# A four-layer graph network on one core: another order for the first full round of the attention ring, and for VectorE's opening

## The chip, the cores and the metric

One core of a Trainium2 chip runs the whole network in one launch. The metric is the device time of a run in microseconds (us). Engines are named as the profile names them: PE (TensorE, with PEld for its weight loads), DVE (VectorE), ACT (ScalarE), POOL (GpSimd) and SP (SyncE, which here only issues DMAs). Each engine executes its own queue strictly in order; an instruction that waits holds up everything behind it on that engine and nothing on the others.

## The reference, cut to what matters

Input x has shape (128, 64, 256): 128 graphs of 64 nodes with 256 features, and one 64x64 adjacency for all. Four layers follow each other, each of the form x = x + layer(relu(layernorm(x))):

```python
# layer 0: aggregation with the normalized adjacency, then two products with batch norms
A_norm = A + I;  dinv = rsqrt(row sums + column sums - diagonal)
agg = (A_norm * dinv[:, None] * dinv[None, :]) @ h
out = batchnorm(relu(batchnorm(agg @ W1.T + b1)) @ W2.T + b2)
# layer 1: two graph convolutions, then LSTMs over windows of 1, 2, 3 and 4 nodes
# layer 2: causal attention with one head of 256, adjacency added to the scores
# layer 3: attention with 4 heads of 64, masked where the adjacency is 0; the output keeps its layout
```

All is float32.

## The kernel before, in words

The 8192 rows of x are cut into 16 chunks of 512 rows (four tiles of 128 rows and 256 features). Layer 0 goes over the chunks twice (the batch norms need sums over all chunks), layer 1 over pairs of chunks. Layers 2 and 3 are one software pipeline, which the code calls a ring: while chunk c is in layer 2, chunk c-2 gets its projections in layer 3 and chunk c-3 its softmax. This study touches two places: the opening, and the first full round of that ring.

**The opening** (lines 376 to 409). A manual schedule: all five engines execute in the order in which the code is written. The adjacency and the first two chunks of x are loaded; the first chunk comes in two halves, one issued by SP (L382) and one by ACT (L383). `degrees` (L119 to L122) makes the row sums on DVE; `rsqrt` (L99, L100) makes dinv on POOL. `normalized` scales the rows by dinv on DVE (L129), transposes them on PE (L131) and scales again on DVE into `ahat_t` (L132). `ln_stats` takes each tile's mean and variance on DVE (L159, L160) and the inverse deviation on POOL (L99, L100); `ln_apply` makes the shift `nmr` on DVE (L172) and normalizes on ACT, tile by tile, into `hs` (L174). `aggregate0` multiplies `hs` by `ahat_t` on PE (L201) and copies one half of the result on DVE (L332) and one on ACT (L334). `product1` makes the first product on PE (L347), copies it out on ACT (L349) and takes the batch norm's sums on DVE (L350). `keep_busy` issues transposes of the identity on PE whose results nobody reads (L151). `product1(0)` aggregates the second chunk halfway (L341). From the second chunk on only PE's order is written by hand; that of the other engines is made by the planner that compiles the kernel, from the dependences and its own due times.

**The ring** (lines 1519 to 1561). Each order is a string of steps, `step+k` or `step-k`, run for chunk c+k or c-k; again all five engines follow the order of the string. `FIRST` starts the pipeline with chunks 0 to 2, `ROUND` is one full round, `NORM` and `LAST` end it. The first full round is c = 3. The steps of this study:

- `q2` projects the chunk's queries in two products (L1108); the first half is copied by ACT (L1169), the second by DVE in `copyq2` (L1174). `v2a`, `v2b` and `v3a`, `v3b` project the values (L1101) and copy them by ACT (L1103). `score2` multiplies them (L1191); DVE adds the mask (L1194) and takes the maxima (L1115), POOL subtracts (L1116), ACT exponentiates in `exp2` (L1201). `divide2` is three DVE instructions (L1120, L1125, L1126), `turn2` transposes on PE (L1135) with a copy by ACT (L1139), `out2` multiplies by the values (L1222), and DVE adds to x (L1225).
- `norm3`, `apply3`, `square3`, `load3`: the layer norm's moments on DVE with `rsqrt` on POOL; the shift on DVE (L172) and the normalization on ACT (L174); a transposition in four DVE instructions (L259) that SP writes to DRAM (L234); and SP's reading back (L241), which turns the chunk to channels.
- `qa`, `q5`, `qb`, `qc`, `qd` are seven products for queries and keys (L1297, Strassen's form), accumulated in three PSUM banks X, Y, Z. Bank X is used four times: `qa` copies it by ACT (L1312), `qb` adds to it and copies (L1326), `qc` adds to it and DVE adds it to `qk` (L1336), `qd` adds to it and ACT copies (L1341). Each addition to X waits until the reader before it is done. `c11`, `c12` are DVE's additions of Z and Y. `sums_h` makes four sums of operands on POOL (L674 to L677), after POOL made the sums of the weights in `ring_places` (L1276).
- `exp3`, `sum3`, `divide3`, `turn3`, `out3` are the softmax of layer 3 and its product (L1404, L1120, L1125 and L1126, L1135, L1424); `score3` its scores (L1376, masks L1382).

Of the kernel before, what the change touches and what calls it, by code (L numbers as in the profile page):

```python
# [19 lines left out]
def kernel(  # L20
# [22 lines left out]
    nc = tc.nc  # L43
# [13 lines left out]
    SUP = 2  # L57
# [28 lines left out]
    def bank(name, tag="ps"):  # L86
        return psum[0][0].tile([P, CH], F32, tag=tag, name=name, bufs=psum[0][1][tag])
# [9 lines left out]
    def rsqrt(dst, src, eps):  # L97

        nc.gpsimd.tensor_scalar(dst, src, eps, None, op0=OP.add)  # L99
        nc.gpsimd.tensor_tensor(dst, dst, mhalf[:, : dst.shape[1]], OP.pow)  # L100
# [7 lines left out]
    ahat_t = const.tile([P, P], F32, name="ahat_t")  # L108
# [18 lines left out]
    def normalized(setup, an, dinv):  # L127
        rows = setup.tile([P, P], F32, name="rows")
        nc.vector.tensor_scalar(rows, an, dinv, None, op0=OP.mult)  # L129
        pt = bank("pt_ahat")  # L130
        nc.tensor.transpose(pt[:, :P], rows, ident)  # L131
        nc.vector.tensor_scalar(ahat_t, pt[:, :P], dinv, None, op0=OP.mult)  # L132

    def masks(setup):
        causal = setup.tile([P, P], F32, name="causal")
# [11 lines left out]
    def keep_busy(n, name):  # L147

        ps = bank(f"idle_{name}")
        for i in range(n):  # L150
            nc.tensor.transpose(ps[:, :P], ident, ident)  # L151


    def ln_stats(src, name, tiles=range(NJ)):
        n = len(tiles)
        st = small.tile([P, n, 6], F32, tag=f"ln_st{n}", name=f"st_{name}")
        mv = small.tile([P, n, 2], F32, tag=f"ln_mv{n}", name=f"mv_{name}")
        for i, j in enumerate(tiles):
            nc.vector.bn_stats(st[:, i, :], src[:, j, :])  # L159
            nc.vector.bn_aggr(mv[:, i, :], st[:, i, :])  # L160
        rstd = small.tile([P, n], F32, tag=f"ln_rstd{n}", name=f"rstd_{name}")
        rsqrt(rstd, mv[:, :, 1], EPS)
        return mv, rstd

    def ln_apply(dst, src, mv, rstd, name, tiles=range(NJ), by_pool=False):
        n = len(tiles)
        nmr = small.tile([P, n], F32, tag=f"ln_nmr{n}", name=f"nmr_{name}")
        if by_pool:
            nc.gpsimd.tensor_tensor(nmr, mv[:, :, 0], rstd, OP.mult)
            nc.gpsimd.tensor_scalar(nmr, nmr, -1.0, None, op0=OP.mult)  # L170
        else:
            nc.vector.scalar_tensor_tensor(nmr, mv[:, :, 0], -1.0, rstd, op0=OP.mult, op1=OP.mult)  # L172
        for i, j in enumerate(tiles):
            nc.scalar.activation(dst[:, j, :], src[:, j, :], AF.Relu, bias=nmr[:, i : i + 1],  # L174
                                 scale=rstd[:, i : i + 1])
# [15 lines left out]
    def aggregate(src, mat, name):  # L191

        banks = [bank(f"agg{e}_{name}").rearrange("p (k j t) -> p k j t", j=NJ, t=T) for e in range(2)]
        for j in range(NJ):
            for k in range(KD):
                for i in range(2):
                    for e in range(2):
                        f = slice(k * P + i * T, k * P + (i + 1) * T)  # L200
                        nc.tensor.matmul(banks[e][half(i), k, j, :], src[half(e), j, f],  # L201
                                         mat[half(e), half(e)], start=True, stop=True)
        return [ps.rearrange("p k j t -> p (k j) t") for ps in banks]
# [105 lines left out]
    setup, close_setup = pool("setup", 1, "right")  # L309
# [17 lines left out]
    def aggregate0(c):  # L327
        aggs[c] = l0.tile([P, KD, CH], F32, tag="agg", name=f"agg_{c}")
        dst = aggs[c].rearrange("p k (j e t) -> p e (k j) t", e=2, t=T)
        for e, ps in enumerate(aggregate(hs.pop(c), ahat_t, f"a{c}")):  # L330
            if e == 0:
                nc.vector.tensor_copy(dst[:, e], ps)  # L332
            else:
                nc.scalar.copy(dst[:, e], ps)  # L334
# [39 lines left out]
    with tc.manual_schedule(engines={mybir.EngineType.PE, mybir.EngineType.DVE,  # L374
                                     mybir.EngineType.Activation, mybir.EngineType.Pool,
                                     mybir.EngineType.SP}):
        for e in range(2):
            r = slice(e * T, (e + 1) * T)
            nc.sync.dma_start(adj_bd[r, r], adj)
            nc.scalar.dma_start(adjt_bd[r, r], adj_t)  # L380
        xts = [l0.tile([P, NJ, D], F32, tag="xt", name=f"xt_{c}", bufs=3) for c in range(2)]
        nc.sync.dma_start(xts[0][:, : NJ // 2], xr[0][:, : NJ // 2])  # L382
        nc.scalar.dma_start(xts[0][:, NJ // 2 :], xr[0][:, NJ // 2 :])  # L383
        nc.gpsimd.dma_start(w1_sb, w1t.rearrange("(k p) f -> p k f", p=P))
        nc.sync.dma_start(xts[1], xr[1])
        for c in range(2):
            hs[c] = l0.tile([P, NJ, D], F32, tag="h", name=f"h_{c}")
        nc.sync.dma_start(bn1_sb, bn1)
        others = setup.tile([P, P], F32, name="others")
        nc.vector.tensor_scalar(others, ident, -1.0, 1.0, op0=OP.mult, op1=OP.add)  # L390
        dinv = degrees(setup, others)
        keep_busy(34, "a")

        parts = [range(2 * i, 2 * i + 2) for i in range(2)]
        stats = [ln_stats(xts[0], "a00", parts[0])]
        an = setup.tile([P, P], F32, name="an")
        nc.vector.tensor_add(an, adj_bd, ident)
        normalized(setup, an, dinv)
        keep_busy(10, "b")
        stats.append(ln_stats(xts[0], "a01", parts[1]))  # L400
        for i in range(2):
            ln_apply(hs[0], xts[0], *stats[i], f"a0{i}", parts[i])
        mv, rstd = ln_stats(xts[1], "a1")
        aggregate0(0)
        ln_apply(hs[1], xts[1], mv, rstd, "a1")
        keep_busy(8, "c")
        xt = load0(2)
        stats2 = xt, *ln_stats(xt, "a2")
        product1(0)
# [563 lines left out]
    st, steps = {}, {}  # L973
# [530 lines left out]
    def store(c, t):  # L1504
# [3 lines left out]
        for r in range(2):  # L1508
# [5 lines left out]
    ROUND = """exp3-3 q2+0 copyq2+0 sum3-3 load3-1 sums_h-2 load2+1 v2a+0 divide3-3 score2+0 exp2+0 v2b+0  # L1514
               divide2+0 turn3-3 qa-2 turn2+0 q5-2 c11-2 out2+0 keep+0 norm3a+0 qb-2 back-2 qc-2 norm3b+0 c12-2
               v3a-2 qd-2 apply3+0 out3-3 score3-2 store-3 square3+0 v3b-2"""

    NORM = """exp3-3 q2+0 copyq2+0 sum3-3 load3-1 sums_h-2 v2a+0 divide3-3 score2+0 exp2+0 v2b+0 norm2+1
              divide2+0 turn3-3 qa-2 turn2+0 q5-2 c11-2 out2+0 keep+0 norm3a+0 qb-2 apply2+1 back-2 qc-2
              norm3b+0 c12-2 v3a-2 chan2+1 qd-2 apply3+0 out3-3 score3-2 store-3 square3+0 v3b-2"""  # L1520
# [5 lines left out]
               score2+1 norm3+0 exp2+1 q2+2 divide2+1 copyq2+2 apply3+0 back+0 v2a+2 v2b+2 turn2+1  # L1526
               score2+2 chan3+0 pair1+14 pair1+14 out2+1 keep+1 exp2+2 divide2+2 q30+0 k30+0 turn2+2
               norm3+1 pair1+15 pair1+15 q31+0 k31+0 apply3+1 out2+2 keep+2 square3+1 score3+0 norm3+2
               v3a+0 load3+1 v3b+0 apply3+2 square3+2"""
    LAST = """exp3-2 sum3-2 load3+0 divide3-2 qa-1 q5-1 c11-1 v3a-1 qb-1 c12-1 qc-1 turn3-2 out3-2 qd-1  # L1530
              q30+0 score3-1 store-2 back-1 k30+0 back+0 exp3-1 q31+0 k31+0 sum3-1 divide3-1 score3h+0
              v3b-1 exp3a+0 sum3a+0 turn3-1 exp3b+0 v3a+0 divide3a+0 out3-1 sum3b+0 divide3b+0 store-1
# [3 lines left out]
    def run(order, c):  # L1536
        for name in order.split():
            i = max(name.find("+"), name.find("-"))
            steps[name[:i]](c + int(name[i:]))

    with tc.manual_schedule(engines={mybir.EngineType.PE, mybir.EngineType.DVE,
                                     mybir.EngineType.Activation, mybir.EngineType.Pool,
                                     mybir.EngineType.SP}):
        run(FIRST, 0)
        close_l1r()
        pool3, close_l3 = pool("l3", 2, "right")
        l3.append(pool3)
# [58 lines left out]
```

## Time and profile before

| | us |
|---|---|
| median of 8 runs | 1925.62 (1923.12 to 1927.42) |
| the profiled execution's own time | 1926.83 |
| its span, first to last instruction | 1925.1 |
| PE busy in the span | 1901.7 (99%) |
| DVE busy | 1159.2 (60%) |
| ACT busy | 958.3 (50%) |
| POOL busy | 413.1 (21%) |

The mean granted clock of TensorE over the span is 0.998 of full speed. A row of the timeline has the start in us from the span's start, the duration (of merged instructions from the first start to the last end), engine, line, operation, tiles, shapes and count, and in brackets how long the engine had been idle and what ended that. Matmuls are pipelined: a row's end lies some 0.1 to 0.2 us behind the start of the row that follows it without a gap, so distances on PE are taken from start to start.

### The profile page before, as it was taken

To read this page: it belongs to the slowest core of one execution; us is meant where nothing else is said; L and a number is where in the kernel's file an instruction comes from. 1 tells how busy PE (TensorE), PEld (TensorE's weight loads), DVE (VectorE), ACT (ScalarE), POOL (GpSimd) and SP (SyncE) were. 2 spreads that over 40 slices of the span, in tenths; PEclk is the share of its full clock that TensorE was granted. 3 is DMA by queue.
4 is the path that set the end of the run, shared out by engine and by line. 5 is a ranking of instruction groups with operands and counts; after the bars stand their busy time and mean duration, and the time that the engine had idled before them with its cause. 6 is when DMAs were issued, how large, how long until landed. Compare 5 with 4: busy or idle time off the path is not lost.

```text
span 1925.1 us, 38314 instructions
## 1 busy us (share of the span) xinstructions
PE 1901.7 (99%) x14979; PEld 1464.5 (76%) x14979; DVE 1159.2 (60%) x3019; ACT 958.3 (50%) x2132; POOL 413.1 (21%) x613
## 2 busy tenths in 40 slices
PE   9999999999999999999999999999999999999998
PEld 5444465897897889699689789878969967777776
DVE  6644354546557656755755764665555566677776
ACT  5655434445455455455545645545554544444453
POOL 3204210221211221121121121112113113233332
PEclk9999999999999999999999999999999999999999
DMA  4116712224424521532632452353144244444433
GB/s 135 60 40 221 276 53 66 83 83 163 155 83 148 180 95 64 178 103 91 194 135 83 159 181 83 104 184 107 56 143 131 87 150 137 133 141 147 143 111 111
DMA packets 110500, 240.36 MB, mean 125 GB/s; under 512 B 11376, under 2 KB 74352, under 8 KB 110320
## 3 DMA queue, kind: packets, MB, share of 16 engines
q1 hardware_dynamic: 109568, 236.57, 36.9%
q8 instruction: 119, 1.95, 0.4%
q0 software_dynamic: 320, 1.05, 0.2%
q14 instruction: 61, 0.50, 0.1%
q10 hardware_dynamic: 432, 0.30, 0.0%
HBM read 169.98 MB, written 67.90 MB: 124 GB/s over the span
## 4 chain that ended last, share of the span: by engine, by line
PE 95%; DVE 3%; ACT 1%; issue 1%; POOL 0%; DMA 0%; SPq 0%; DVEq 0%; POOLq 0%; ACTq 0%
PE x L829 22%; PE g L793 18%; PE z L829 11%; PE z L347 6%; PE y L829 6%; PE z L364 6%; PE v L1101 5%; PE p_q L1108 3%; PE u L574 3%; PE v L560 3%; PE X L1297 3%; PE Y L1297 1%; PE agg_a L201 1%; PE agg_c L201 1%; PE s L1191 1%; PE agg_b L201 1%
## 5 line engine op out<-in xcount | busy, mean ns | idle before, releaser
L838 DVE TENSOR_TENSOR gates<-gates,x 128x128 f32<-128x128 f32 (+2 forms) x384 | 119.5, 322 | 335.4 <-PE x L829 328.4
L829 PE MATMUL x<-xd,wset 128*128 128x128 f32 (+2 forms) x1280 | 285.6, 311 | 0.4 <-DVE gates L838 0.2
L829 PE MATMUL x<-hd,wset 128*128 128x128 f32 (+2 forms) x1152 | 247.2, 303 | 0.0
L829 PEld LDWEIGHTS x<-xd,wset 128*128 128x128 f32 x1280 | 202.4, 190 | 17.5 <-DVE gates L838 3.9
L887 POOL TENSOR_TENSOR gates<-gates 128x512 f32<-128x512 f32 (+2 forms) x48 | 74.9, 1560 | 648.1 <-ACT gates L721 648.1
L721 ACT ACTIVATE gates<-gates,bias 128x256 f32<-128x256 f32 (+4 forms) x384 | 170.4, 491 | 67.0 <-DVE gates L838 64.3
L829 PEld LDWEIGHTS x<-hd,wset 128*128 128x128 f32 x1152 | 185.3, 191 | 4.9
L772 ACT ACTIVATE gates<-g,bias 128x512 f32<-128x512 f32 (+2 forms) x240 | 138.0, 609 | 98.0 <-PE g L793 94.7
L793 PE MATMUL g<-hT,wset 128*128 128x256 f32 (+2 forms) x744 | 184.5, 405 | 1.2 <-DVE hT L732 1.1
L793 PEld LDWEIGHTS g<-hT,wset 128*128 128x128 f32 x744 | 140.9, 190 | 43.8 <-issue 8.8
L793 PE MATMUL g<-hT,wih 128*128 128x512 f32 x384 | 166.4, 593 | 0.0
L835 ACT COPY gates<-y 128x128 f32<-128x128 f32 (+2 forms) x192 | 54.1, 293 | 205.4 <-PE y L829 204.9
L829 PE MATMUL z<-hs,wset 128*128 128x128 f32 (+2 forms) x768 | 154.3, 303 | 0.0
L793 PEld LDWEIGHTS g<-hT,wih 128*128 128x128 f32 x384 | 72.5, 191 | 87.5 <-issue 83.1
L829 PEld LDWEIGHTS z<-hs,wset 128*128 128x128 f32 x768 | 119.9, 191 | 3.3
L347 PE MATMUL z<-agg,w_sb 128*128 128x512 f32 x256 | 114.1, 599 | 0.1
L778 DVE TENSOR_TENSOR cell<-gates 128x512 f32<-128x512 f32 (+2 forms) x80 | 50.4, 647 | 101.4 <-ACT gates L772 101.3
L364 PE MATMUL z<-h,w_sb 128*128 128x512 f32 x256 | 110.2, 593 | 0.0
L838 DVE TENSOR_TENSOR gates<-gates,z 128x128 f32<-128x128 f32 (+2 forms) x384 | 104.8, 317 | 0.1
L835 ACT COPY gates<-x 128x128 f32<-128x128 f32 (+2 forms) x192 | 56.5, 295 | 93.9 <-PE x L829 93.1
L721 ACT ACTIVATE gates<-x,bias 128x128 f32<-128x128 f32 (+2 forms) x192 | 74.7, 389 | 50.9 <-PE x L829 48.0
L829 PE MATMUL z<-hT,wset 128*128 128x128 f32 (+1 forms) x512 | 97.0, 302 | 0.0
(243 smaller groups left out, 3646.5 us busy)
## 6 DMA issues: line engine op xcount, KB each, us to landing
wset<-wfar SPq DMA_DIRECT2D x96, 960.0 KB, 6.4
hT<-far_h SPq DMA_DIRECT2D x124, 128.0 KB, 2.9
far_h<-hm SPq DMA_DIRECT2D x16, 512.0 KB, 3.7
far_n<-xs SPq DMA_DIRECT2D x16, 512.0 KB, 6.8
xs<-far_n SPq DMA_DIRECT2D x64, 128.0 KB, 3.3
far_x<-xs SPq DMA_DIRECT2D x16, 512.0 KB, 3.0
x<-far_x SPq DMA_DIRECT2D x64, 128.0 KB, 3.2
xt<-in_x_dram SPq DMA_DIRECT2D x15, 512.0 KB, 4.0
```

The costliest lines, as they stand in the source:

```text
L201: nc.tensor.matmul(banks[e][half(i), k, j, :], src[half(e), j, f], mat[half(e), half(e)], start=True, stop=True)
L347: nc.tensor.matmul(ps, w1_sb[:, k, m * P : (m + 1) * P], agg[:, k, :], start=(k == 0), stop=(k == KD - 1))
L364: nc.tensor.matmul(banks[c, m], w2_sb[:, k, m * P : (m + 1) * P], h1[c][:, k, :], start=(k == 0), stop=(k == KH - 1))
L721: nc.scalar.activation(gate(q, c, part), src, AF.Tanh if q == 2 else AF.Sigmoid, bias=bs[:, q * KD + c : q * KD + c + 1])
L772: nc.scalar.activation(columns_of(gate(q, c)), natural(banks[q, c][:, :n].rearrange("p (w b) -> p w b", b=nb)), AF.Tanh if q == 2 else AF. ...
L793: nc.tensor.matmul(banks[q, c][:, :n].rearrange("p (w b) -> p w b", b=nb)[:, w, :], block(q, c, k), hv[:, k, w.start * p : (w.stop - 1) * ...
L829: nc.tensor.matmul(folded(self.psum(kind)), wsets[p, self.q][:, BLOCKS[kind][i], :], (ox[self.s] if part == "x" else oh)[kind], start=firs ...
L835: nc.scalar.copy(gate(self.q, kind // 5, halves[kind // 5]), self.psum(kind))
L838: nc.vector.tensor_add(gate(self.q, *dst), gate(self.q, *a), self.psum(kind))
L887: nc.gpsimd.tensor_mul(gates[:, 0, :, :n], gates[:, 0, :, :n], gates[:, 2, :, :n])
L1101: nc.tensor.matmul(ps[:, i, :], hT[:, k, j, :], w[:, k, first : first + D], start=(k == 0), stop=(k == KD - 1))
L1297: nc.tensor.matmul(st[c, tag][:, i * CH // 2 : (i + 1) * CH // 2].rearrange("p (a n) -> p a n", n=P), w, st[c, "o7"][kind], start=first an ...
```

## The change

Two edits.

In the opening, the second half of the first chunk gets its moments from a generator, `ln_moments`, which does what `ln_stats` does but can be stopped after each tile. One tile's moments now come before `an` (L396) and the scaled rows, the other behind them. `normalized` returns the PSUM bank of its transposition, and the last scaling into `ahat_t` is issued behind the first `ln_apply`. `keep_busy` "b" issues 12 transposes instead of 10. The moments of the second chunk are taken in two halves, one before the aggregation of the first chunk and one behind it, and applied in two halves.

In the ring, `apply3` and `square3` of chunk 2 leave the end of `FIRST`. Round c = 3 gets an order of its own, `THIRD`, in place of `ROUND` with its first three steps permuted: there `apply3` of chunk 2 stands behind `copyq2`, `square3` behind `exp2`, `load2` of chunk 4 ahead of the writing back of `square3`, `sum3`, `load3` and `sums_h` behind `score2` and `exp2`, `turn3` behind `qa`, and `v3a` of chunk 1 behind `qa` instead of behind `c12`.

```diff
+    def ln_moments(src, name, tiles):
+        n = len(tiles)
...
+        for i, j in enumerate(tiles):
+            nc.vector.bn_stats(st[:, i, :], src[:, j, :])
+            nc.vector.bn_aggr(mv[:, i, :], st[:, i, :])
+            yield
+        rstd = small.tile([P, n], F32, tag=f"ln_rstd{n}", name=f"rstd_{name}")
+        rsqrt(rstd, mv[:, :, 1], EPS)
+        yield mv, rstd
...
         stats = [ln_stats(xts[0], "a00", parts[0])]
+        late = ln_moments(xts[0], "a01", parts[1])
+        next(late)
         an = setup.tile([P, P], F32, name="an")
         nc.vector.tensor_add(an, adj_bd, ident)
-        normalized(setup, an, dinv)
-        keep_busy(10, "b")
-        stats.append(ln_stats(xts[0], "a01", parts[1]))
+        pt = normalized(setup, an, dinv)
+        keep_busy(12, "b")
+        next(late)
+        stats.append(next(late))
+        ln_apply(hs[0], xts[0], *stats[0], "a00", parts[0])
+        nc.vector.tensor_scalar(ahat_t, pt[:, :P], dinv, None, op0=OP.mult)
+        ln_apply(hs[0], xts[0], *stats[1], "a01", parts[1])
+        stats = [ln_stats(xts[1], "a10", parts[0])]
+        aggregate0(0)
+        stats.append(ln_stats(xts[1], "a11", parts[1]))
         for i in range(2):
-            ln_apply(hs[0], xts[0], *stats[i], f"a0{i}", parts[i])
-        mv, rstd = ln_stats(xts[1], "a1")
-        aggregate0(0)
-        ln_apply(hs[1], xts[1], mv, rstd, "a1")
+            ln_apply(hs[1], xts[1], *stats[i], f"a1{i}", parts[i])
...
+    THIRD = """q2+0 copyq2+0 apply3-1 exp3-3 load2+1 v2a+0 score2+0 exp2+0 square3-1 sum3-3 load3-1 sums_h-2
+               v2b+0 divide3-3 divide2+0 qa-2 v3a-2 turn3-3 turn2+0 q5-2 c11-2 out2+0 keep+0 norm3a+0 qb-2
+               back-2 qc-2 norm3b+0 c12-2 qd-2 apply3+0 out3-3 score3-2 store-3 square3+0 v3b-2"""
...
-               v3a+0 load3+1 v3b+0 apply3+2 square3+2"""
+               v3a+0 load3+1 v3b+0"""
...
-        run(ROUND.replace("exp3-3 q2+0 copyq2+0", "q2+0 copyq2+0 exp3-3"), SUP + 1)
+        run(THIRD, SUP + 1)
```

More of the change, by code (lines that the diff above doesn't have):

```diff
@@ L131, in normalized @@
         nc.tensor.transpose(pt[:, :P], rows, ident)
-        nc.vector.tensor_scalar(ahat_t, pt[:, :P], dinv, None, op0=OP.mult)
+        return pt
     def masks(setup):
@@ L163, in ln_stats @@
         return mv, rstd
+    def ln_moments(src, name, tiles):
+        n = len(tiles)
+        st = small.tile([P, n, 6], F32, tag=f"ln_st{n}", name=f"st_{name}")
+        mv = small.tile([P, n, 2], F32, tag=f"ln_mv{n}", name=f"mv_{name}")
+        for i, j in enumerate(tiles):
[5 more added lines that the diff above has]
+        yield mv, rstd
     def ln_apply(dst, src, mv, rstd, name, tiles=range(NJ), by_pool=False):
```

## The prediction

> **What bounds the kernel.** I read first the page's table of engines, then the windows around the ring's start, then the timeline there, then the opening. The table says that PE is busy in 99% of the span:
>
> ```profile
> PE 1901.7 (99%) x14979; PEld 1464.5 (76%) x14979; DVE 1159.2 (60%) x3019; ACT 958.3 (50%) x2132; POOL 413.1 (21%) x613
> ```
>
> So only PE's 23.4 us of idleness (1925.1 - 1901.7), and time in which it is slow, can be won. The windows (length, busy time of PE, PEld, DVE, ACT, POOL, granted clock, DMA share, GB/s) find both at the first full round:
>
> ```profile
> 1590.00:1597.00 7.00, 4.05 (x17) 2.35 (x15) 3.75 (x12) 3.68 (x7) 6.66 (x10) 0.92 0.25 75
> 1597.00:1603.00 6.00, 6.00 (x43) 5.07 (x44) 4.33 (x8) 0.99 (x3) 1.78 (x3) 0.53 0.63 201
> ...
> 1615.00:1638.00 23.00, 23.00 (x274) 17.71 (x275) 16.20 (x34) 10.50 (x20) 6.57 (x8) 1.00 0.46 139
> ```
>
> PE loses 2.95 us to idleness, and then runs at a granted clock of 0.53. The shortfalls of both windows, (0.08 x 7 + 0.47 x 6) x 2, make some 6.8 us at half clock. The next round (third line) has neither. The timeline shows the cause:
>
> ```profile
> 1591.68 1.89 PE L1101 MATMUL v<-wvo_sb,hT 128*128 128x256 f32 x8
> ...
> 1592.48 0.72 POOL L1276 TENSOR_TENSOR ws<-w_sb 128x256 f32<-128x256 f32 x1
> 1592.54 0.68 DVE L172 SCALAR_TENSOR_TENSOR nmr_n<-mv_n,rstd_n 128x4 f32<-128x4 f32 x1 [1.47 <-POOL rstd_n L100]
> ...
> 1593.32 2.07 ACT L174 ACTIVATE h<-xs,nmr_n,rstd_n 128x256 f32<-128x256 f32 x4 [4.29 <-DVE nmr_n L172]
> ...
> 1594.93 1.43 DVE L259 STREAM_TRANSPOSE mid<-h 128x256 f32<-128x256 f32 x4 [1.71 <-ACT h L174]
> 1595.30 0.56 ACT L1169 COPY q<-p_q 128x512 f32<-128x512 f32 x1
> ...
> 1596.28 0.65 DVE L1174 COPY q<-p_q 128x512 f32<-128x512 f32 x1
> ...
> 1596.99 1.98 PE L1191 MATMUL s<-hT,q 128*64 128x64 f32 x30 [0.60 <-DVE q L1174]
> ```
>
> The scores wait for the two copies of q2, and these stand, on ACT behind apply3 and on DVE behind square3, both of chunk 2, whose shift waits for POOL. Their product was ready long before (its eight matmuls start at 1588.24).
>
> **The ceiling in the ring.** From the start of q2's products to that of v3b, PE takes 26.60 us here (1588.24 to 1614.84) and 20.50 in the next round (1616.67 to 1637.17). Of the difference of 6.10, 4.26 have arisen by the start of v2b (10.65 against 6.39), 1.75 between v2b and turn3 (half clock, 3.58 against 1.83), 0.09 later.
>
> **The round with the new order.** The starts up to 1588.24 stay. ACT's copy of q2 falls to about 1590.0, copyq2 to 1591.7 (0.04 after the product's end), so the scores start behind v2a at 1593.5 without a wait, and v2b at 1594.6. apply3 keeps its time: its shift waits for POOL until 1592.5 in both versions. qa and v3a fill PE from 1596.5 to 1599.9 (0.87 + 0.86 + 1.73). DVE meanwhile: mask and maxima to 1595.7 (0.42 each), square3 to 1597.1 (1.43), sum3 to 1598.3 (1.21), reciprocal to 1598.6 (0.25), then the multiplication of 1.23 (these are the durations of the same instructions before). Undisturbed it would end at 1599.86, just in time for turn3 at 1599.92.
>
> It is disturbed. POOL now subtracts the second layer's maxima (to 1596.4) ahead of sums_h, whose four additions (0.72 to 0.73 each, 2.90 from 1595.34 to 1598.24 before) move to 1596.4 to 1599.3. The shift at 1592.54 took 0.68 instead of the usual 0.15 to 0.16 and ended 0.02 after POOL's addition beside it; both read two operands from SBUF. The multiplication of divide3 also reads two. I let it wait for the last addition: end at 1600.53, **turn3 0.68 late**. The bounds are 0 and 0.85 (one addition, plus the margin that I may have misplaced). [...]
>
> divide2 follows (0.42 + 0.18 + 0.43) and holds turn2 for another **0.16**. ACT's copies for out2 then end in time; the 0.10 that the next round loses at that place is in the 20.50 and comes back.
>
> v3a is gone from between qc and qd. What it hid:
>
> ```profile
> 1609.19 1.11 PE L1297 MATMUL X<-td,ws 128*128 128x256 f32 x4
> ...
> 1610.13 1.89 PE L1101 MATMUL v<-w_sb,hT 128*128 128x256 f32 x8
> ...
> 1610.40 0.69 DVE L1336 TENSOR_TENSOR qk<-qk,X 128x512 f32<-128x512 f32 x1 [0.52 <-PE X L1297]
> ```
>
> qd writes to bank X, which DVE reads until 1611.09. Without v3a it could start at 1610.13, and it will start at about 1611.16: **1.03 lost**. The bounds are 0 and 1.73, v3a's length. Behind qd on PE wait out3, score3 and v3b, that is, the rest of the round.
>
> The DMAs: load2 of chunk 4 goes out at about 1592 instead of 1601, four issues ahead of the write of square3, which waits for DVE until 1597.1 (before 1596.39). Its reading back lands some 8 us later (1596.39 to 1602.6 and a landing of 2.9 before), against a need at about 1615, when sums_h of the next round starts. SP's keep, back and store stand behind it as before. I cost this at nothing; without that margin of some 9 us it would be paid one to one.
>
> Gain in the ring: 6.10 + 0.10 - 0.68 - 0.16 - 1.03 = **4.33**. The rounds behind it are bound by PE, so it lasts to the end.
>
> **The opening.** PE's end of the aggregation and DVE's copy set the first product:
>
> ```profile
> 14.16 1.09 PE L151 MATMUL idle_c<-ident 128*128 128x128 f32 x8
> ...
> 14.65 0.66 DVE L332 COPY agg<-agg_a 128x512 f32<-128x512 f32 x1
> ...
> 15.41 3.67 PE L347 MATMUL z<-agg,w_sb 128*128 128x512 f32 x8
> ```
>
> In the new order one tile's moments (0.52) push the scaled rows from 9.16 to 9.68; the transposition starts at 10.02, and the 12 idle transposes (0.108 each) end at 11.5, beside the normalization. The last tile's moments end at 10.63 instead of 11.30, the rsqrt for it at 11.71 instead of 12.40, so ACT normalizes the last two tiles at 11.94 instead of 12.63, and PE ends 0.69 earlier. Two of the second chunk's tiles no longer stand ahead of DVE's copy, which gives 0.16 more: the first product starts at 14.56, **0.85** earlier.
>
> Little of that lasts. Three chunks on, PE waits for the normalization of chunk 3:
>
> ```profile
> 31.08 2.07 ACT L174 ACTIVATE h<-xt,nmr_a,rstd_a 128x256 f32<-128x256 f32 x4 [1.83 <-POOL nmr_a L170]
> ...
> 31.89 1.78 PE L201 MATMUL agg_a<-ahat_t,h 64*64 64x64 f32 x64
> ```
>
> The aggregation takes 1.71 there, from start to start, instead of 1.09, paced by ACT. That normalization hangs on DVE without a break since 23.95, and that on the batch norm's sums of the first product (19.09), ACT-bound before. In the new order DVE waits for POOL's rsqrt of the second half (until 16.6; before 16.21), then does the 2.21 us of chunk 2's moments, and starts those sums at 18.93: 0.16 earlier. So I count **0.16** of the 0.85; the bounds are -0.5 (DVE's wait for POOL 0.5 longer than I place it) and 0.85 (the planner, which orders DVE from the second chunk on, finds another order).
>
> **Sum.** 4.33 + 0.16 = 4.49. Against the profiled execution, 1926.83 (1.73 around its span of 1925.1), that is 1922.3; that execution is 1.21 above the median, and from the median it is **1921.1**.
>
> **Rivals.** (1) DVE's chain and bank X cost nothing and the opening's gain lasts: 6.10 + 0.85 = 6.95, 1918.7. For it: DVE meets turn3 within 0.1 without POOL. Against it: X's accumulation waits in this very round (0.21 for the copy of L1326). Chance 0.20. (2) The clock. Half clock cost 1.75 + 0.77 (scores, 1.90 instead of 1.13) = 2.52 of the 6.10. If the median run lacks it, the gain is 4.49 - 2.52 = 1.97, 1923.7; if the new waits bring it, 6.83 x 0.5 = 3.41 are lost, 1924.5. For it: the runs before spread over 4.3 us. Against it: the new gaps are 0.68 and 1.03, apart by 5 us. [...] Chance 0.15. (3) The wait moves to turn3: DVE's chain there is 1.5 later than I place it, which PE pays one to one: 4.49 - 1.5, 1922.6. Chance 0.12. (4) Slower: the planner's order for layer 0 shifts with the opening, and each later chunk's normalization comes late. From chunk 4 on it is 4.4 us early (ACT ends at 36.3, PE needs it at 40.7), so lateness must pass 4.4; each us beyond costs 12 chunks 12 us. It decides from 5.1: 0.7 x 12 = 8.4 lost, 1929.5; at 5.5 it is 13.2, 1934.3. Nothing but the planner's freedom speaks for it. Chance 0.03. The forecast has 0.50, with 1920.0 to 1922.4 as its own range.
>
> **Range and chances.** What a measurement of this kernel can tell from no change is about 0.2%, 3.85 us: faster means below 1921.77. About three quarters of the forecast lie there (0.37) and all of (1): 0.57. The rest of it, (2) and (3) are the same: 0.40. The range takes in most of (1) and half of (2): 1918.8 to 1923.7.
>
> **What would show it.** Right: after the start of q2's products the scores start within 5.4 us, the granted clock stays at 1.00 in the round; qd starts 2.0 behind qc; divide3's multiplication lasts about 1.9; the first product starts near 14.6, chunk 3's aggregation takes about 2.4. Wrong: a new gap on PE ahead of turn3 of over 1 us, a clock below 0.9 anywhere in the ring, or an aggregation that waits again after chunk 3.

## The result and the profile after

The median of the changed kernel is 1919.42 us (1918.71 to 1921.08, 10 runs), beside 1925.47 us for the kernel before in the same comparison (1922.70 to 1928.54, 28 runs): a ratio of 0.997 [0.9962, 0.9978], or 6.05 us less. The forecast was 1921.1, 4.49 less. The profiled execution took 1919.54 with a span of 1917.7; the one before took 1926.83 with 1925.1.

The two spans differ by 7.31 (unrounded ends). Cut at rows that both traces have, the difference is:

| stretch | before | after | gain |
|---|---|---|---|
| start to DVE's first sum over the adjacency (its DMA has landed) | 6.86 | 6.06 | 0.80 |
| to the mark in layer 0 | 30.28 | 29.85 | 0.43 |
| to layer 1's first product | 233.15 | 233.15 | 0.00 |
| to the start of chunk 3's q2 in the ring | 1317.96 | 1317.10 | 0.86 |
| to the start of PE's last matmul | 331.14 | 326.88 | 4.26 |
| to the end (copies and stores) | 5.66 | 4.70 | 0.96 |

The mark in layer 0 is the ninth of the 16 matmuls of chunk 2's first product, the one right behind chunk 3's aggregation; two of the texts on record call it the fourth chunk's first product. The first and the last row aren't the change's: kernels with the old opening that ran later (e1, e3, e4 and e12 below) had 6.05 to 6.19 and 4.69 to 6.02 there. That leaves 5.55 for the change in this pair of executions.

The table of engines has 4.5 us less on PE:

```profile
PE 1897.2 (99%) x14981; PEld 1461.0 (76%) x14981; DVE 1158.9 (60%) x3020; ACT 958.0 (50%) x2132; POOL 414.1 (22%) x615
```

The same windows as before, laid at the same distance behind the start of q2's products, here 1586.16 (columns: length, busy time of PE, PEld, DVE, ACT, POOL, granted clock, DMA share, GB/s):

```profile
1587.92:1594.92 7.00, 7.00 (x56) 5.24 (x55) 4.60 (x14) 4.25 (x8) 6.30 (x9) 1.00 0.72 152
1594.92:1600.92 6.00, 6.00 (x61) 4.67 (x59) 4.05 (x7) 3.62 (x8) 3.10 (x4) 1.00 0.51 175
```

PE's idle time of 2.95 is gone, and so is the half clock. The timeline of the changed kernel in that round:

```profile
1588.14 0.58 ACT L1188 COPY q<-p_q 128x512 f32<-128x512 f32 x1 [1.19 <-PE p_q L1127]
...
1589.80 0.69 DVE L1193 COPY q<-p_q 128x512 f32<-128x512 f32 x1 [0.80 <-PE p_q L1127]
...
1590.47 0.69 DVE L185 SCALAR_TENSOR_TENSOR nmr_n<-mv_n,rstd_n 128x4 f32<-128x4 f32 x1
...
1591.42 1.20 PE L1210 MATMUL s<-hT,q 128*64 128x64 f32 x32
...
1596.28 1.22 DVE L1145 TENSOR_TENSOR s<-s,rs 128x1024 f32<-128x1024 f32 x1
...
1596.43 1.67 POOL L696 TENSOR_TENSOR td<-hT,td 128x256 f32<-128x256 f32 x1
...
1597.83 1.25 PE L1154 MATMUL tr<-ident,s 128*128 128x128 f32 x10
```

Both copies of q2 now end ahead of the shift, and the scores start 5.26 behind q2 with nothing in brackets: PE did not wait. From q2 to v3b it takes 21.73 (1586.16 to 1607.89) instead of 26.60; the next round takes 20.50 as before. Nor did it wait for turn3: all ten transpositions follow each other. Of the two instructions that the forecast saw in conflict, divide3's multiplication kept its 1.22 and POOL's last addition took 1.67 instead of 0.73.

What is left over the next round's 20.50 is nearly all in one wait:

```profile
1602.78 1.11 PE L1316 MATMUL X<-td,ws 128*128 128x256 f32 x4
...
1604.00 0.69 DVE L1355 TENSOR_TENSOR qk<-qk,X 128x512 f32<-128x512 f32 x1 [0.52 <-PE X L1316]
...
1604.83 1.10 PE L1316 MATMUL X<-td,w_sb 128*128 128x256 f32 x4 [0.94 <-DVE qk L1355]
```

qd starts 2.05 behind qc; in the next round the product behind qc follows it after 0.94, without a wait, so 1.11 is lost.

In the opening, the rows that answer to those before:

```profile
12.82 1.09 PE L151 MATMUL idle_c<-ident 128*128 128x128 f32 x8
12.94 0.69 DVE L345 COPY agg<-agg_a 128x512 f32<-128x512 f32 x1 [0.61 <-PE agg_a L214]
...
13.75 3.66 PE L360 MATMUL z<-agg,w_sb 128*128 128x512 f32 x8
```

Counted from DVE's first sum, the first product starts at 7.69 instead of 8.55. In the profiles of the other kernels with the new opening, told below, it starts at 7.49 to 8.19. Chunk 3's normalization is still late:

```profile
29.86 2.07 ACT L187 ACTIVATE h<-xt,nmr_a,rstd_a 128x256 f32<-128x256 f32 x4 [2.28 <-POOL nmr_a L183]
...
30.51 1.94 PE L214 MATMUL agg_a<-ahat_t,h 64*64 64x64 f32 x64 [0.22 <-ACT h L187]
...
32.38 4.13 PE L360 MATMUL z<-agg,w_sb 128*128 128x512 f32 x9
```

The aggregation takes 1.87 from start to start (1.71 before; without a wait it is 1.09, as for chunk 4 here).

### The profile page after: what moved, and what is told of

Its sections match the earlier page's. It is cut to its first block, busy times and chain, and to the rows that moved or that the text cites. A ratio compares the mean times of both kernels' runs of the same rounds, so it can differ in the third digit from the quotient of the medians.

```text
span 1917.7 us, 38323 instructions
## 1 busy us (share of the span) xinstructions
PE 1897.2 (99%) x14981; PEld 1461.0 (76%) x14981; DVE 1158.9 (60%) x3020; ACT 958.0 (50%) x2132; POOL 414.1 (22%) x615
## 4 chain that ended last, share of the span: by engine, by line
PE 94%; DVE 3%; ACT 1%; DMA 1%; issue 0%; POOL 0%; ACTq 0%; SPq 0%; DVEq 0%; POOLq 0%
PE x L848 23%; PE g L812 18%; PE z L848 11%; PE y L848 6%; PE z L377 6%; PE v L1120 6%; PE z L360 5%; PE p_q L1127 3%; PE u L593 3%; PE v L579 3%; PE X L1316 3%; PE Y L1316 1%; PE agg_c L214 1%; PE o L1241 1%; PE agg_b L214 1%; PE o L1443 1%
```

## The experiments

In the texts on record letters stand for theories; each is said again where its run is told. Every kernel ran beside runs of the kernel before on the same chip.

| kernel | median (range, runs) | ratio to before |
|---|---|---|
| both edits (the change) | 1919.42 (1918.71 to 1921.08, 10) | 0.997 [0.9962, 0.9978] |
| e1 ring alone | 1921.54 (1920.11 to 1924.02, 11) | 0.998 [0.9971, 0.9989] |
| e2 opening alone | 1923.76 (1921.76 to 1924.30, 11) | 0.9988 [0.9979, 0.9997] |
| e3 before, gap filled | 1925.09 (1924.32 to 1926.58, 11) | 0.9995 [0.9986, 1.0004] |
| e4 two steps moved | 1924.84 (1923.89 to 1926.97, 11) | 0.9996 [0.9987, 1.0005] |
| e5 v3a back | 1920.84 (1920.24 to 1921.30, 7) | 0.9975 [0.9964, 0.9986] |
| e6 v3b as cover | 1919.63 (1918.33 to 1920.82, 5) | 0.9967 [0.9955, 0.998] |
| e7 divide3 a little later | 1919.45 (1) | none |
| e8 masks later | 1919.87 (1919.30 to 1920.83, 6) | 0.997 [0.9959, 0.9982] |
| e9 masks in DVE's idle time | 1919.19 (1918.39 to 1920.23, 6) | 0.9966 [0.9954, 0.9978] |
| e10 divide3 behind POOL | 1921.25 (1) | none |
| e11 e9, e6 and the next round | 1917.67 (1917.36 to 1918.78, 5) | 0.9958 [0.9946, 0.9971] |
| e12 ring alone, opening filled | 1921.93 (1921.63 to 1923.49, 11) | 0.9983 [0.9974, 0.9992] |

### The two edits apart

```diff
 e1: the kernel before, with
-        run(ROUND.replace("exp3-3 q2+0 copyq2+0", "q2+0 copyq2+0 exp3-3"), SUP + 1)
+        run(THIRD, SUP + 1)
 (and FIRST without its apply3 and square3); e2: the changed kernel with the ring of before
```

> The new order of the ring's first full round with the opening of before. Theory A (the gain comes from that round: the scores' wait and the half clock that the wait brings): from the start of q2's products to that of v3b 21.7 us as in the changed kernel (before 26.6), granted clock 1.00 in the round, and a time of about 1919.8, that is 0.4 above the changed kernel. Rival B (the opening gives a good part, since the two profiles stand 1.2 us apart after the third chunk and 2.1 us at the ring's start): the same round, but a time of 1921 or more.

> The new opening with the ring of before. Theory A: the first product starts 0.85 us earlier, counted from the landing of the adjacency (the first sum on DVE), but the aggregation of chunk 3 waits for its normalization and leaves 0.4 us; a time 0.4 below before, which hardly shows. Rival B: 1.2 to 2.1 us below before, 1923.4 to 1924.3.

Against the medians of before beside them, the ring alone brought 4.37 us (1925.91 to 1921.54) and the opening alone 2.15; together 6.05. The ring's size is the forecast's (4.33). The opening's isn't: 0.16 was forecast. Theory A's times (1919.8 for the ring alone, 0.4 below before for the opening alone) were not met; rival B, that the opening gives a good part (1921 or more, and 1923.4 to 1924.3), was right on both. In e2's trace the ring is that of before (26.59 from q2 to v3b, with the drop of the clock), and the first product starts at 7.49 behind DVE's first sum. In e1's trace q2 to v3b took 21.72, step for step as in the changed kernel. But its opening, which is that of before, ran differently than in before's own profile: two windows of e1 (columns as above):

```profile
13.27:16.68 3.41, 3.41 (x26) 2.54 (x18) 2.40 (x10) 1.61 (x4) 1.27 (x2) 0.50 0.46 156
...
269.27:272.68 3.41, 3.41 (x24) 2.31 (x23) 3.08 (x11) 0.71 (x2) 1.05 (x3) 0.50 0.03 5
```

Twice the granted clock falls to half for 3.41 us. The mark in layer 0 came 1.24 later than in before's profile (31.52 behind DVE's first sum instead of 30.28), and the stretch from layer 1's first product to q2 took 0.81 more (1318.77 instead of 1317.96). Before's own profile has neither drop; it had its one drop of 6.83 in the ring. So if the opening's new order keeps such drops away, that part of its gain cannot be seen in before's profile; whether it does is asked below.

### The clock

```diff
 e3: the kernel before, with 20 idle transposes ahead of the scores of chunk 3
+    def fill(c):
+        keep_busy(20, "g")
-        run(ROUND.replace("exp3-3 q2+0 copyq2+0", "q2+0 copyq2+0 exp3-3"), SUP + 1)
+        run(ROUND.replace("exp3-3 q2+0 copyq2+0", "q2+0 copyq2+0 exp3-3").replace("score2+0", "fill+0 score2+0"), SUP + 1)
```

> The kernel before with 20 idle transposes on PE (about 2.2 us) between v2a and the scores of round 3, inside the wait of 3.4 us; nothing is moved. Theory A (idleness lowers the clock there, in most executions and not in all): the scores start as late as before, 8.7 us after q2's products, but the granted clock stays at 1.00, v2b takes 1.83 from start to start instead of 3.58, and the median falls by about 2.5 us to 1923.0, with the runs closer together than the 5.8 us of before. Rival C (the clock drops there for another reason, or transposes do not hold it up): clock and time as before. [...]

In e3 q2 starts at 1589.97. Its windows over the gap and behind it:

```profile
1592.00:1599.00 7.00, 6.08 (x42) 4.62 (x42) 3.75 (x11) 3.95 (x7) 6.66 (x10) 1.00 0.27 79
1599.00:1605.00 6.00, 5.79 (x55) 4.93 (x52) 4.05 (x8) 2.09 (x6) 1.51 (x3) 1.00 0.72 209
```

The scores came as late as before (7.68 behind q2), but the clock stayed at 1.00, v2b to turn3 took 1.83 instead of 3.58, and q2 to turn3 11.66 instead of 14.23: 2.57 less, where the prediction priced the half clock at 2.52. So the clock's half of the ceiling is shown by itself: the wait stayed and the half clock went. Of the median's 2.5 us to 1923.0, which were expected with it, only 0.8 came, and the interval takes in no change. This profile has drops at 13.58 and 269.58 as e1's has, and the runs fall into two groups: 1924.3 to 1925.1 at a listed clock of 0.998 or 0.999, and 1926.2 to 1926.6 at 0.997. Why the better group gains so little is open.

In a trace with several changes of the clock they lie on one grid. In e1 the two drops are 256.00 apart, in before the first rise (8.61) and the drop (1595.81) 1587.20, and that drop lasts 6.83: 75.0, 465.0 and 2.0 times 3.413 (each of e1's drops lasts 3.41). The phase of that grid against the kernel differs from execution to execution (the drops at 269.27 in e1 and at 269.58 in e3, both with the old opening). The window ahead of a drop in the ring had PE busy for 1.17 of 3.41 us (before), 1.19 (e2) and 0.69 (e4); ahead of the drops at 13 and 269 it was 1.95 to 2.21, and such values passed elsewhere without a drop (2.17 in before, 2.04 in e5), so these rows give no sharp threshold. No window ahead of one of these drops was idle throughout. (The traces of before and after also end in a drop, at 1923.49 and 1917.38, behind the end of PE's last matmuls at 1919.61 and 1913.26; there PE is done.)

Of the profiled executions with the old opening and no filler (before, e1, e3, e4), three dropped at 13 or 269 or both; of nine with the new one, none. All three drops at 269 came where the grid lay 0.82 to 1.76 ahead of layer 1's first product, and no execution with the new opening had it there. So the new opening may avoid the drops, or may only have shifted the work against the grid. e12 fills the gaps with the old opening kept:

```diff
 e12: e1, with more idle transposes ahead of the first aggregation and of layer 1
-        keep_busy(10, "b")
+        keep_busy(20, "b")
-            for at, fill, name in ((6, 16, "d"), (9, 6, "e"), (10, 6, "f")):
+            for at, fill, name in ((6, 26, "d"), (9, 6, "e"), (10, 6, "f")):
```

> The opening of before with the new round in the ring, and 10 more idle transposes (about 1.1 us each) at two places where PE is idle for 1.1 us: ahead of the first aggregation (10 to 20), and ahead of layer 1's first aggregation (16 to 26). No other engine's order changes. Theory L (with the opening of before, these gaps lower the clock for a window of 3.4 us at 13.3 and at 269 us in a good part of the executions, which the new opening avoids): no granted clock below 1.00 before the end, runs closer together than the 3.9 us of the ring alone, and a median about 1 us lower, 1920.5. Rival M (the lower clock there has nothing to do with these gaps): windows at half clock at the same places, 1921.5.

Its profile has no drop (the same two windows):

```profile
13.27:16.68 3.41, 3.23 (x44) 2.10 (x37) 2.40 (x10) 1.30 (x3) 1.28 (x2) 1.00 0.44 135
...
269.27:272.68 3.41, 3.04 (x10) 1.42 (x9) 2.43 (x8) 1.19 (x3) 1.69 (x4) 1.00 0.03 5
```

By itself this profile decides nothing: its grid lay against the work nearly as before's did (first rise at 8.59 and 8.61; 2.06 and 2.26 ahead of layer 1's first product), and before had no drop at 13 or 269 either. The runs say more: all 11 list a clock of 0.999 or 1.000, where three of e1's list less and are its three slowest; the spread is 1.9 us instead of 3.9. So the filler does seem to keep such drops away, as L had it. L's median of 1920.5 did not come (1921.93 against e1's 1921.54, in two comparisons). One reason is in the trace: the mark in layer 0 comes at 30.86 instead of 30.28, without a drop at 13. It isn't the longer filler: that ends just as the first aggregation starts. The clock rose only at 8.59, so the idle transposes ahead of the transposition, which e12 has as before, ran slowly until then (in before 0.213 us apart ahead of its rise at 8.61 and 0.109 behind it), ended only at 9.49 and held it up (3.27 behind DVE's first sum instead of 2.64). In before they ended as late, but DVE's first sum came at 6.86 there and at 6.05 here.

The drops explain the long runs of e1, not the distance of the medians: e1's eight runs at 0.999 and 1.000 have a median of 1921.29. What stays between the changed kernel (1919.42) and e1 or e12 is some 2 us, of which the profiles show 1.0 at the mark in layer 0 (29.85 against 30.86 in e12) and 0.82 between layer 1 and the ring (1317.10 against 1317.92). That last piece is the same in all nine executions with the new opening (1317.08 to 1317.17) and, between before and after, arises at three places of layer 1: 0.36 at 267.9 behind layer 1's first product, 0.34 at 868.7 and 0.18 at 1112.6. The order of instructions on each engine is the same in that stretch before and after, so the planner did not choose another one. No run here explains it; it stays open.

### The round, step by step

```diff
 e4: the kernel before, apply3 and square3 of chunk 2 moved, nothing else
+        run(ROUND.replace("exp3-3 q2+0 copyq2+0", "q2+0 copyq2+0 apply3-1 square3-1 exp3-3"), SUP + 1)
 e5: the changed kernel, v3a of chunk 1 behind c12 again
+        run(THIRD.replace("qa-2 v3a-2", "qa-2").replace("c12-2 qd-2", "c12-2 v3a-2 qd-2"), SUP + 1)
```

> The kernel before, where only apply3 and square3 of chunk 2 move from the end of FIRST behind copyq2; the rest of round 3 keeps the order of ROUND (sums_h ahead of the second layer's subtraction, sum3 and divide3 ahead of the scores' mask, v3a behind c12). Theory A: the scores start at once, but PE has only v2b ahead of turn3 and waits there some 2.6 us for divide3; qd does not wait. 4.87 - 2.6 + 1.1 = 3.4 us gained, 1922.1, if the new wait does not lower the clock, and about 1924 if it does. Rival D (the other moves of the round do nothing): as the ring alone, about 1919.8.

e4 undoes the wait that the prediction began with, and the scores start 5.25 behind q2, as in the changed kernel. But the round comes out at 25.14, 1.46 less than before, because the wait reappears:

```profile
1600.15 1.94 PE L1135 MATMUL tr<-ident,s 128*128 128x128 f32 x8 [2.87 <-DVE s L1126]
```

PE waits 2.87 for divide3 (2.6 was expected), and the clock drops at 1600.00 for 3.41. The median, 1924.84, lies near the 1924 that was expected with such a drop, though its interval takes in no change; rival D, that the other moves do nothing (1919.8), is ruled out. So the other moves of the new order together carry more than half of the ring's gain (21.73 against 25.14): qa and v3a ahead of turn3, sums_h behind the second layer's subtraction, and the mask ahead of sum3. Only v3a is taken apart from them, by e5.

> The changed kernel, with v3a of round 3 back between c12 and qd. Theory E (v3a covers one of two waits, here or there): qd follows v3a without a wait, but PE is at turn3 1.73 us earlier and waits there some 1.7 us for divide3's multiplication, so the round gets 1.73 - 1.11 = 0.6 us longer: from the start of q2's products to that of v3b 22.3 us instead of 21.73. Rival F (v3a gains nothing ahead of turn3): the wait of qd, 1.1 us, is simply saved: 20.6.

In e5 qd doesn't wait, and turn3 does:

```profile
1598.06 1.41 PE L1154 MATMUL tr<-ident,s 128*128 128x128 f32 x10 [1.39 <-DVE s L1145]
```

q2 to v3b takes 22.25 (22.3 was expected): at its new place v3a covers the wait of turn3 (PE would be there at 9.94 behind q2 and starts at 11.49, so 1.55, of which the row lists 1.39 as idle), at its old place the 1.1 of qd's. Its new place is the better one by 0.52 in the trace; the median is 1.42 above that of the change, in another comparison.

### Which of two engines is held

> The changed kernel with one DVE instruction more, a second reciprocal of the sums (about 0.25 us, its result unused) ahead of divide3 in round 3, so that the multiplication of divide3 comes behind the start of POOL's last addition of sums_h instead of 0.15 us ahead of it. Theory H (whichever of the two starts first holds the other, as the shift beside ring_places shows): the multiplication lasts about 1.9 us instead of 1.22, POOL's addition 0.73 instead of 1.67, and turn3 comes 0.6 us late: q2 to v3b 22.3 us. Rival I (only POOL is held, DVE never): the multiplication starts 0.28 later, still lasts 1.22, turn3 is not later than 0.1: 21.8. [...]

```diff
 e7 and e10: reciprocals whose result is not used ahead of divide3 of chunk 0 (one in e7, three in e10)
+        for i in range(3):
+            nc.vector.reciprocal(small.tile([P, NJ * HEADS], F32, tag="again", name="again"), st[c, "sm3"])
-        run(THIRD, SUP + 1)
+        run(THIRD.replace("divide3-3", "again-3 divide3-3"), SUP + 1)
```

One reciprocal moved the multiplication by 0.12 only; it still started 0.04 ahead of POOL's addition, lasted 1.23, and the addition 1.77. The run tells nothing on the order that was asked about. e10 has three:

> As the run with one more reciprocal ahead of divide3, which moved the multiplication only from 10.12 to 10.24 us behind q2's products, still ahead of POOL's last addition (10.28); here three more, so that it comes at about 10.6, inside that addition (10.3 to 11.0). Theory H (the second to start is held): the multiplication lasts 1.5 to 1.65 us instead of 1.22, POOL's addition 0.73 instead of 1.67, turn3 12.2 behind q2's products instead of 11.67. Rival I (only POOL is held): the multiplication lasts 1.22 and turn3 comes at 11.9.

The timeline of e10:

```profile
1596.21 0.73 POOL L696 TENSOR_TENSOR td<-hT,td 128x256 f32<-128x256 f32 x1
...
1596.40 1.62 DVE L1145 TENSOR_TENSOR s<-s,rs 128x1024 f32<-128x1024 f32 x1
...
1598.16 1.06 PE L1154 MATMUL tr<-ident,s 128*128 128x128 f32 x8 [0.39 <-DVE s L1145]
```

Now POOL's addition is 0.19 ahead and lasts 0.73, and the multiplication lasts 1.62 and holds turn3, which comes at 12.21 behind q2 (11.67 in the changed kernel). H, that whichever of the two starts second is held, was right (1.5 to 1.65, 0.73 and 12.2); I, that the multiplication keeps its time, was wrong. In the changed kernel the multiplication was 0.15 ahead and POOL's addition took 1.67, so this pair of runs shows it from both sides. The prediction had the multiplication held, and so the wrong order. Both kernels ran once, so their times say nothing here.

### Where the opening's gain went, and where more was to be had

> The changed kernel, where the masks (five DVE instructions, 0.82 us from 23.94 to 24.76 in its profile, and one of POOL) and the load of layer 0's second weights are issued after the third chunk's first product instead of before the second's. Theory J (the opening's gain is held back by DVE's chain to the normalization of chunk 3): that normalization comes 0.8 us earlier, PE's aggregation of chunk 3 takes 1.1 us from start to start instead of 1.87, the fourth chunk's first product starts 0.78 earlier counted from the first sum on DVE, and the time falls by as much, to 1918.7. Rival K (the planner fills the place with other work, or another engine bounds it): no change.

> The changed kernel, where the masks stand in the opening's hand-written order, behind the shift of chunk 2, where DVE is idle for 2.7 us (in the run before this one the planner put them back to their old place). Theory J (the opening's gain is held back by DVE's chain to the normalization of chunk 3): that chain gets 0.8 us shorter, PE's aggregation of chunk 3 takes 1.1 us from start to start instead of 1.87, the fourth chunk's first product starts about 28.9 us behind the first sum on DVE instead of 29.7 to 29.85, and the time falls by 0.7 to 1918.7. Rival K (something else holds that normalization, or a later aggregation waits instead): no change.

```diff
 e8: masks(setup) and what follows it issued behind product1(3); e9: ahead, in product1(0):
                 ln_apply(hs[2], *stats2, "a2")
+                masks(setup)
...
-        masks(setup)
         close_setup()
```

J was that the masks' copies, which the planner puts on DVE at 23.94 to 24.76 in the changed kernel, stand in the chain of chunk 3's normalization. In e8 the planner put them at the same place again (23.55 to 24.35), so nothing was tested; the mark in layer 0 came at 29.70. In e9 they fall into DVE's idle time earlier on, and PE's aggregation waits no more:

```profile
8.63 0.43 DVE L171 BATCH_NORM_STATS2 st_a<-xt 128x6 f32<-128x256 f32 x1 [0.62 <-DMA xt<-in_x_dram]
...
30.66 1.27 PE L214 MATMUL agg_a<-ahat_t,h 64*64 64x64 f32 x64
31.86 4.56 PE L361 MATMUL z<-agg,w_sb 128*128 128x512 f32 x10
```

1.20 from start to start instead of 1.87. J was right on the chain. The 0.7 us of time isn't shown: e9's median is 0.23 below that of the change, within the intervals. In this execution the load of chunk 0's second half landed late (first row), and the mark in layer 0 came at 29.39; e11, with the same edit, has 28.76, which is 1.09 ahead of the changed kernel's.

That first row shows a wait that the prediction had no term for. The new order needs chunk 0's second half earlier, and DVE waits for its load by 0.29 in e5, 0.48 in e6 and 0.62 in e9. Where the load was in time (e2, e7, e10), the first product starts at 7.49 and the mark comes at 29.66, 0.62 ahead of before; in e6 it comes at 30.27, where before had 30.28. So a part of the opening's gain hangs on when this load lands.

```diff
 e6: v3b between c12 and qd, where v3a had been
+        run(THIRD.replace("square3+0 v3b-2", "square3+0").replace("qc-2 norm3b+0 c12-2", "qc-2 norm3b+0 c12-2 v3b-2"), SUP + 1)
 e11: e9 and e6, and the round after it with the copies of q2 ahead of exp3
+        run(ROUND.replace("exp3-3 q2+0 copyq2+0", "q2+0 copyq2+0 exp3-3"), SUP + 2)
```

> The changed kernel, with v3b of chunk 1 taken from the end of round 3 and put between c12 and qd, where nothing covers qc's addition on DVE. Theory E: qd's wait of 1.11 us (qc to qd 2.05 from start to start, 0.94 without a wait) goes: from q2's products of round 3 to those of round 4 22.4 us instead of 23.56, and a time of about 1918.3. Rival G (ACT's copy of v3b ahead of qd's copy, or the scores ahead of round 4, cost as much): 23.0 or more, no change in time.

> The changed kernel with the masks in DVE's idle time, v3b of round 3 between c12 and qd, and round 4 with q2 and copyq2 ahead of exp3 (with v3b moved alone, the 1.3 us of round 3 came back as a wait of round 4's scores for ACT's copy of q2, which stands behind exp3 there). Theory E: round 3 takes 22.3 us from q2 to q2 and round 4's scores start 5.3 us behind its q2 as in the changed kernel; turn3 of round 4 waits some 0.3 us; 0.9 us gained there and 0.7 in the opening: 1917.8. Rival G (the exponentials come late and the wait moves on to turn3 or to round 5): 1918.7, the masks' share alone.

v3b covers qd's wait: q2 to the next round's q2 takes 22.27 instead of 23.56 (22.4 was expected by theory E). But the time is G's, unchanged (1919.63), because e6 gives most of it back at once, as the ring did before the change:

```profile
1613.50 1.06 ACT L1423 ACTIVATE s<-s 128x1024 f32<-128x1024 f32 x1 [3.54 <-POOL s L1135]
...
1614.46 0.57 ACT L1188 COPY q<-p_q 128x512 f32<-128x512 f32 x1
...
1615.08 1.09 PE L1210 MATMUL s<-hT,q 128*64 128x64 f32 x29 [0.83 <-ACT q L1188]
```

The next scores wait for ACT's copy of q2 behind exp3. With that copy ahead of exp3 (e11) all 32 score matmuls follow each other:

```profile
1610.81 1.89 PE L1120 MATMUL v<-wvo_sb,hT 128*128 128x256 f32 x8
1612.63 1.61 PE L1210 MATMUL s<-hT,q 128*64 128x64 f32 x32
```

though they take 1.54 up to v2b instead of 1.13. The scores start 5.36 behind that q2 (5.3 expected). e11 has the lowest median of all kernels here: 1917.67, 1.75 below that of the change; 1917.8 was expected. The two were measured in two comparisons, and the intervals of their ratios overlap a little.

## Why the prediction was right, step by step

**The ring's ceiling** of 6.10 was right: 4.87 of it was had at v3b, and of the 1.23 left over the next round 1.11 is qd's wait. e3 shows the price of the clock alone (2.57 against 2.52).

**turn3 and turn2** (0.68 and 0.16 lost) were wrong, both 0. The failed step is "I let it wait for the last addition". That one would hold the other was the author's estimate from one row, the shift's 0.68 instead of 0.16. POOL's addition was placed at 1598.6 (1599.3 less 0.72) and the multiplication at 1598.6 as well, and the choice between them was a toss that the profile could not decide; DVE came 0.15 ahead. The size for the other order was near: e10's multiplication lost 0.40 and turn3 0.54.

**qd** (1.03 lost): 1.11. The mechanism and the wait's releaser are as forecast. **The DMAs** (nothing): none of the round's waits on PE names one. The prediction's way to its 8 us, over 1602.6 and a landing of 2.9, misreads the trace: square3's data were back at 1603.50 in the profile before, 7.1 us behind the start of their write (6.9 in the changed kernel). With the margin of some 9 us it changes nothing.

**Sum of the ring**, 4.33: 4.87 at v3b, 4.26 at PE's last matmul (4.37 between medians of e1). Two errors met. Ahead of v3b 0.84 too much was charged; without it the sum would have been 5.17, of which 0.3 did not come (0.08 more at qd, the 0.10 that was to come back, and small gaps). And "so it lasts to the end" was not quite true, which took 0.5 to 0.6. That the sum came out within 0.1 of the medians is luck in part. In the fourth round PE pauses with nothing to wait for:

```profile
1630.22 0.70 PE L1120 MATMUL v<-w_sb,hT 128*128 128x256 f32 x2
1631.15 1.45 PE L1120 MATMUL v<-w_sb,hT 128*128 128x256 f32 x6 [0.23 <-issue]
```

and a lead of 6.95 at v3b is 6.56 at the start of chunk 5's q2 and 6.35 at the last matmul. Other kernels with the same ring lose other amounts there (326.06 to 327.36 from q2 to the last matmul); what sets them isn't shown.

**The opening's first product** (0.85 earlier): 0.86. That **0.16** of it lasts was too low: 0.43 at the mark in this pair, 0.62 in e2, e7 and e10, and 0.01 in e6, where the load came late. The named chain (chunk 3's normalization behind DVE's unbroken work) is right, e9 cuts it. In this pair the size was off: chunk 3's normalization follows 1.22 ahead of its place before (29.86 against 31.08), 0.42 of which is left when the common shift of 0.80 is taken off; the two sums of the first product on DVE no longer wait for ACT between them (1.26 together against 1.44), which the working had left out. **Not in the prediction at all** are the drops of the clock in the opening and the 0.8 us between layer 1 and the ring. The profiles show these two beside the 0.43, and no more is known of the 2.15 that the opening brought alone. So the total is larger than forecast (6.05 for 4.49) because of the opening, by causes that are in part open, and not because of the ring.

**The signs.** Met were the scores (5.26 for 5.4 at most), the clock, qd (2.05 for 2.0) and the first product's 0.86. Missed were the multiplication (1.22 for 1.9) and chunk 3's aggregation (1.87 for 2.4). No later aggregation of layer 0 waits.

**Rivals.** (1), everything hidden, 1918.7, lies nearer to the median than the forecast (0.7 against 1.7). Of its three claims one held: turn3 cost nothing, but qd did, and the opening's gain lasted by half at the mark in layer 0. (2): the clock does weigh in the runs before. By the clock listed for each, those beside e1 to e4 took 1924.3 at 0.999, 1926.1 at 0.998, 1927.2 at 0.997 and 1928.3 at 0.996 (means), about 1.3 us for each 0.001; but it worked the other way round: the runs after list 0.999 and 1.000, so the change lost none of the clock's share and probably gained some. (Single runs of e5, e6 and e9 list 0.998.) (3) is what e4 and e5 make, not the change. (4) did not happen: layer 0 to layer 1 took 233.15 in both.

## What to carry to other kernels

A wait that goes shows the next one: e4 took away the right wait and gained little, because the work that covers the following one had not been moved with it, and e6 repeated that one round later. Where an instruction of one engine is held by one of another, as the multiplication and POOL's addition were here (1.62 instead of 1.22, 1.67 instead of 0.73), and the two arrive within some 0.2 us of each other, give both orders as cases, not the one that the sum happens to give. One profile of a kernel with idle stretches on PE shows one position of the clock's grid only (with the same opening, before's had no drop at 13 or 269 and e1's had both); the spread of the runs and the clock listed for each say whether other positions cost more.

## What the runs showed of the hardware

In the traces with several changes of the clock they lay on a grid of 3.413 us (256.00 in e1, 1587.20 and 6.83 in before) whose phase differed between executions (269.27 in e1, 269.58 in e3). A drop inside the work lasted one or two steps of it (3.41 in e1 and e4, 6.83 in before), and PE had not been idle for a whole step ahead of any of these (busy 0.69 to 2.21 of 3.41). Idle transposes alone brought the clock to 1.00 in the opening (at 5.92 in the changed kernel, ahead of any other matmul; they followed each other by 0.213 us until then and by 0.109 behind it), and with 20 of them ahead of the scores it stayed at 1.00 in e3; the profile lists them as MATMUL with the identity. Of DVE's multiplication and POOL's addition the one that started second was held for about the rest of the first: POOL's 0.73 became 1.67 behind a multiplication that had started 0.15 ahead (0.94 longer, with 1.07 of the multiplication left), DVE's 1.22 became 1.62 behind an addition that had started 0.19 ahead (0.40 longer, with 0.54 left). An instruction that waited held up what stood behind it on its engine: in before ACT's normalization waited 4.29 for the shift, and the copy of q2 behind it started 7.06 behind q2's products, where it started 1.98 behind them in the changed kernel, ahead of that normalization. PE and POOL started other work in that wait (1591.68 and 1592.48).
